# A two-layer attention block on one core: another order for layer 0's output projection of the first batch, and for vector work beside attention

## The chip, the cores and the metric

The kernel runs on one core of one Trainium2 chip. The metric is the time of one execution on the device, in microseconds (us), taken as the median of several runs. One execution was also recorded by the hardware profiler. The core has five engines, each of which works through its own queue in order: TensorE (PE, matrix products), VectorE (DVE), ScalarE (ACT), GpSimd (POOL), and SyncE (SP), which here only issues transfers. Engines wait for each other by semaphores.

## The reference, cut to what matters

The input `x` has 8 images of 32×32 positions with 512 channels, all in fp32. Two residual layers follow one another:

```python
x = x + L0(_gn(x), w_qkv, w_proj, b_proj)
x = x + L1(_gn(x), Wq, Wk, Wv, Wo, pos_emb_w, pos_emb_h)

def _gn(v, G=32, eps=1e-5):       # mean and variance over an image and 16 channels
    ...
def L0(x, w_qkv, w_proj, b_proj): # 16 heads of 32 channels, 1024 tokens
    q, k, v = split(x @ w_qkv)
    attn = softmax((q * 32 ** -0.5) @ k.T)
    return (attn @ v) @ w_proj + b_proj
def L1(x, Wq, Wk, Wv, Wo, pos_emb_w, pos_emb_h):  # 4 heads of 128 channels
    q, k, v = x @ Wq * 128 ** -0.5, x @ Wk, x @ Wv
    attn = softmax(q @ k.T + relative_logits(q, pos_emb_w, pos_emb_h))
    return (attn @ v) @ Wo
```

## The kernel before, in words

**Projections.** Every product with a 512×512 weight matrix is a Strassen-Winograd product: seven factor products of half size stand for eight. Four sums of blocks of the moving operand are needed for them, made on DVE by `forming` (lines 339 to 362; `forms` runs it through): s1 = a21 + a22, s2 = s1 − a11, a21 := a11 − a21, s4 = a12 − s2. Products 0 and 1 take a11 and a12 as they are, product 3 takes a22, and products 5, 4, 6 and 2 take s2, s1, the new a21 and s4. The like sums of the weights are made by POOL once at the start (`Matrix.add_up`) and stored to DRAM. A projection is done in two units u, one for each half of the output channels. `seven` (line 390) issues a unit: product 0 into the PSUM bank x, which ACT copies out as p1; product 5 into bank y, to which DVE adds p1, giving a (line 411); product 1 into x; product 4 into y, from which DVE makes b (line 419); product 6 into bank z, copied by ACT as p7; then products 2 and 3. A product that reuses a bank waits for the reader of what was there. Sinks take the results; the sink `Onto` adds them to the residual, with a POOL addition for the parts that come by a snapshot (line 502) and DVE additions for the others (lines 507 and 509). `two_first` and `five_last` (lines 437 to 475) issue products 0 and 1 of a unit and the other five apart; before, only the last batch's WO uses them.

**Layer 0's attention** (`attention_0`, line 595) goes over four groups of heads (m), two halves of the tokens (h) and eight blocks of keys (j). A step issues `front` of block j and then `back` of block j − 1. `front`: matmuls ps (line 603), then the exponential e on ACT (line 611). `back`: matmuls acc (line 622), then DVE's running sum es (line 631 for the first two blocks, line 633 for the others). ps has one PSUM buffer and e two, so that ACT's exponential of block j must wait until DVE has added block j − 2 to es, and the matmuls of block j + 1 must wait for that exponential. At the end of a half the sum over keys is made by a matmul (line 643), and the result normalised by ACT, DVE and at last POOL (line 588, q times su).

**What stands beside it.** The main loop goes through b = 0 to 8. Beside layer 0's attention of batch b it puts, in a chain: the output projection WP of batch b − 1 with its residual (`after_0`, line 891); layer 1's output projection WO of batch b − 2 (`after_1`), woven with the group norm of batch b − 1 (`norm_1`, line 905); layer 1 of batch b − 1 (`second`, line 910, projections Wq, Wk, Wv, and `attention_1`), woven with the loading and the group norm of batch b + 1 (`load`, line 786); and layer 0's projections of batch b + 1 (`before_0`). For the first batches, where some of these don't exist, the place is taken by others: `rest_of_first` finishes batch 0's projections beside the load of batch 1, and `other_keys` the second unit of batch 1's keys beside batch 0's norm.

A group norm is: statistics of a chunk of 128 channels (bn_stats, line 259; bn_aggr, line 260); a chain of DVE operations on a few columns ("small operations", lines 285 to 296, from `turned` to `var`); the power on POOL (line 300); four normalisations of 128×1024 (line 304). The residual is stored to DRAM before it is normalised (`put_away`, line 223, tile d) and fetched again for the next addition (`fetch`, line 232, into x1T or x2T).

**What sets the order.** All parts are generators, which yield after a piece of work with its cost in matmuls. `side_by_side` issues pieces of the chain beside the attention's steps in proportion to these costs. `woven(main, side, start, gap, places)` takes one piece of `side` at those pieces of `main` whose number, less `start`, leaves a remainder in `places` when divided by `gap`. In-order queues do the rest: the framework puts each engine's instructions in an order near that of issue, and `tc.issue_after(x)` keeps an instruction behind x. Weight factors come by SP (`Stream`, line 200 and 204) in the order of `plan`, seven factors ahead, through 16 buffers, and all other transfers of SP stand in the same queue.

Of the kernel before, what the change touches and what calls it, by code (L numbers as in the profile page):

```python
# [27 lines left out]
def quick_path(  # L28
# [23 lines left out]
    nc = tc.nc  # L52
# [265 lines left out]
    begun = [None]  # L318
    half_done = [None]

    added = [None]

    def by_columns(out, weights, moving, start, stop, open_sum=False):
# [12 lines left out]
                tc.keep_in_program_order(ins)  # L336
        in_place[0] = False

    def forming(x, name, room=None, behind=None):


        a11, a12 = x[:, :HC, :NB], x[:, HC:, :NB]
        a21, a22 = x[:, :HC, NB:], x[:, HC:, NB:]
        if room is not None:
            s1, s2, s4 = [room[:, i, :].rearrange("p (c n) -> p c n", n=NB) for i in range(3)]
        else:
            s1, s2, s4 = [
                mem.tile([P, HC, NB], F32, tag=f"form{i}", name=f"f{i}_{name}", bufs=1)
                for i in (1, 2, 4)
            ]  # L350
        for op, out, one, other in (
            (nc.vector.tensor_add, s1, a21, a22),
            (nc.vector.tensor_sub, s2, s1, a11),
            (nc.vector.tensor_sub, a21, a11, a21),
            (nc.vector.tensor_sub, s4, a12, s2),
        ):

            late = behind() if behind is not None else None
            with tc.issue_after(late.ins) if late is not None else nullcontext():
                last_form[0] = op(out, one, other)  # L360
            yield 0
        return [a11, a12, s4, a22, s1, s2, a21]

    def forms(x, name, room=None):
        got = []
# [31 lines left out]
    def seven(fs, u, rows, sink, name, hook=None):  # L397

        product = taken(fs, u, rows)
        x = bank(f"x_{name}")
        product(x, 0, True)
        p1 = snapshot("e1", f"p1_{name}")
        nc.scalar.copy(p1, x)
        yield HC
        y = bank(f"y_{name}")
        product(y, 5, True)
        a = snapshot("es1", f"a_{name}")  # L410
        begun[0] = nc.vector.tensor_add(a, y, p1)
        sink.early(p1, a)
        yield HC
        product(x, 1, False)
        sink.c11(x)
        yield HC
        product(y, 4, False)
        b = snapshot("es1", f"b_{name}")
        half_done[0] = nc.vector.tensor_add(b, y, p1)
        sink.middle(b)  # L420
        yield HC
        z = bank(f"z_{name}")
        product(z, 6, True)
        p7 = snapshot("e1", f"p7_{name}")
        nc.scalar.copy(p7, z)  # L425
        yield HC
        product(y, 2, False)
        sink.c12(y, p1)
        if hook is not None:
            hook()  # L430
        yield HC
        product(z, 3, False)
        sink.c21(z, a)
        sink.c22(b, p7)
        yield HC

    def two_first(fs, u, sink, name):

        product = taken(fs, u, False)
        x = bank(f"x_{name}")  # L440
        product(x, 0, True)
        p1 = snapshot("e1", f"p1_{name}")
        nc.scalar.copy(p1, x)
        product(x, 1, False)
        sink.c11(x)
        return p1

    def five_last(fs, u, sink, name, p1):
        product = taken(fs, u, False)
        y = bank(f"y_{name}")  # L450
        product(y, 5, True)
        a = snapshot("es1", f"a_{name}")
        nc.vector.tensor_add(a, y, p1)
        sink.early(p1, a)
        product(y, 4, False)
        b = snapshot("es1", f"b_{name}")
        nc.vector.tensor_add(b, y, p1)
        sink.middle(b)
        z = bank(f"z_{name}")
        product(z, 6, True)  # L460
        p7 = snapshot("e1", f"p7_{name}")
        nc.scalar.copy(p7, z)
        product(y, 2, False)
        sink.c12(y, p1)
        product(z, 3, False)
        sink.c21(z, a)
        sink.c22(b, p7)

    class Plain:

# [119 lines left out]
    def attention_0(q, k, v, b, blocks=range(NT)):  # L590
# [23 lines left out]
        def back(m, h, j, e):  # L614
            name = f"0_{b}_{m}_{h}_{j}"
            if j == blocks[0]:
                state["acc"] = psum.tile([P, NB], F32, tag="acc", name=f"acc_{name}", bufs=1)
                state["first"] = e
            acc = state["acc"]
            for r in range(HB):  # L620
                c0 = (m * HB + r) * D0
                nc.tensor.matmul(  # L622
                    acc[r * D0 : (r + 1) * D0, :],
                    v[:, j, c0 : c0 + D0],
                    e[:, r, :],
                    start=(j == blocks[0]),
                    stop=(j == blocks[-1]),
                )
            if j == blocks[1]:
                state["esum"] = mem.tile([P, HB, NB], F32, tag="es0", name=f"es_{name}", bufs=1)  # L630
                nc.vector.tensor_add(state["esum"], state["first"], e)  # L631
            elif j != blocks[0]:
                nc.vector.tensor_add(state["esum"], state["esum"], e)  # L633
            if j != blocks[-1]:
                return
            nc.scalar.copy(q[m][:, h * NB : (h + 1) * NB], acc)
            state["ended"] = (m, h, state["esum"])
# [149 lines left out]
    def load(b, st):  # L787
# [18 lines left out]
        yield 0  # L806
        st["kept"] = put_away(xT, f"0_{b}")
        yield from group_norm(st, xT, f"0_{b}")
        st["xn"] = yield from forming(x, f"xn0_{b}", behind=lambda: added[0])

    def load_first(st):

# [63 lines left out]
    def before_0(b, st, hook=None):  # L876
# [1 line left out]
        fs = st["xn"]  # L878
        st["q0"] = block(f"q0_{b}")
        st["q"] = chunks(st["q0"])  # L880
        yield from project_T(fs, WQ0, st["q"], f"q0_{b}")
        st["k"] = chunks(block(f"k0_{b}"))

        yield from project_T(fs, WK0, st["k"], f"k0_{b}", (0,) if b == 1 else (0, 1))
# [5 lines left out]

    def after_0(b, st, hook=None):

        fs = st.pop("ao0") if "ao0" in st else forms(st["q0"], f"ao0_{b}", block(f"forms_{b}"))
        x = st["x1"] = block(f"x1T_{b}")
        xT = fetch(st["kept"], x)
        for u in range(2):
            bias = [bproj_sb[:, n * HC + u : n * HC + u + 1] for n in range(2)]
            stream.unit(WP, False, u)
            yield from seven(
                fs, u, False, Onto(halves(xT, u), bias), f"wp_{b}_{u}", hook if u else None  # L900
            )
            for n in range(2):
                statistics(st, xT, n * HC + u, f"1_{b}")

    def norm_1(b, st, after=None, behind=None):
        xT = chunks(st["x1"])
        st["kept"] = put_away(xT, f"1_{b}")
        yield from group_norm(st, xT, f"1_{b}", after, behind)

    def second(b, st):  # L910

        fs = forms(st.pop("x1"), f"xn1_{b}")
        q = st["ao"] = block(f"q1_{b}")
        yield from project_T(fs, WQ1, chunks(q), f"q1_{b}")
        posT = block(f"posT_{b}", dtype=F32R)
        k = chunks(block(f"k1_{b}"))
        v = block(f"v1_{b}", [P, NT, C])
# [50 lines left out]
    def after_last(b, st):  # L968
# [1 line left out]
        x = st["ao"]  # L970
        xT = fetch(st["kept"], block(f"x2T_{b}"))
        sinks = [Onto(halves(xT, u), then=put_out(b, st, xT, u)) for u in range(2)]
        early = [x[:, :HC, :NB], x[:, HC:, :NB]]
        p1s = []
        for u in range(2):
            stream.unit(WO, False, u)
            p1s.append(two_first(early, u, sinks[u], f"wo_{b}_{u}"))
        fs = forms(x, f"ao1_{b}")
        for u in range(2):
            stream.unit(WO, False, u)  # L980
            five_last(fs, u, sinks[u], f"wo_{b}_{u}", p1s[u])

    def woven(main, side, start, gap, places=(0,)):

# [26 lines left out]
    def chain(*parts):  # L1011
        for part in parts:
            yield from part

    def marked():
        in_place[0] = True
        return
        yield
# [12 lines left out]
    def units(m, rows=False):  # L1031
        return [(m, rows, u, ORDER) for u in range(2)]

    FIRST = units(WQ0) + units(WK0) + units(WV0, True)
    plan = [(m, m is WV0, u, ORDER) for u in range(2) for m in (WV0, WQ0, WK0)]
    for b in range(B + 1):
        if b >= 1:
            plan += units(WP)
        if b == 1:
            plan += units(WK0)[1:]  # L1040
        if b >= 2:
# [2 lines left out]
            plan += units(WQ1) + units(WK1) + units(WV1, True)  # L1044
        if b + 1 < B:
            plan += FIRST if b else units(WQ0) + units(WK0)[:1] + units(WV0, True)
    plan += [(WO, False, u, some) for some in (FIRST_TWO, LAST_FIVE) for u in range(2)]

    states = [{} for _ in range(B)]
    load_first(states[0])  # L1050
# [21 lines left out]
    for b in range(B + 1):  # L1072
# [10 lines left out]

        if last is not None:
            if past is not None:
                norm = norm_1(b - 1, last, after=lambda: half_done[0])
            else:
                norm = norm_1(b - 1, last, behind=lambda: begun[0])
            rest.append(after_0(b - 1, last, forms_past if past is not None else None))
            total += PRODUCT  # L1090
            if past is not None:
                rest.append(woven(later(after_1, b - 2, past), norm, 3, 3))
                total += PRODUCT
            else:
                rest.append(chain(woven(other_keys(b, here), norm, 0, 1), marked()))
                total += PRODUCT // 2
            rest.append(later(second, b - 1, last))
            total += SECOND
# [14 lines left out]
                incoming = later(late_output, past)  # L1113
            rest.append(woven(attention, incoming, 4, 5))
        else:
            rest.append(woven(rest_of_first(here), incoming, 0, 2))
            total += PRODUCT
        if coming is not None:

# [502 lines left out]
```

## Time and profile before

| quantity | us |
|---|---|
| median of three runs | 3848.02 (3847.01 to 3848.98) |
| the profiled execution | 3848.35 |
| its span, first to last instruction | 3846.6 |
| PE busy | 3789.4 |
| DVE busy | 2555.1 |
| ACT busy | 1760.2 |
| POOL busy | 621.6 |

The span is what the trace covers; 1.75 us of the profiled execution lie around it. Busy shares are averages over the span. In a line of the timeline, the first number is the start from the span's beginning, the second the duration (of all instructions of the group, where x16 or the like stands behind it), then engine, line of the code, operation, output <- inputs with their shapes, and in brackets the idle time of the engine just before, with what ended it. In a line of waits: engine, what it issued <- what it waited for, the total in us, how many times, the longest. Batch 0's layer 0 runs up to about 310 us, and from b = 2 on one round of the main loop takes some 471 us.

### The profile page before, as it was taken

The numbers are of one execution on the slowest core, as the hardware profiler recorded it, in microseconds if no ns is written. First come the engines' busy times: TensorE is split into PE (matmuls) and PEld (weight loads), VectorE is DVE, ScalarE is ACT, GpSimd is POOL, SyncE is SP. The second block draws the span as 40 slices with busy tenths as digits, with TensorE's granted clock in tenths as the row PEclk, the third lists the DMA queues.
The fourth block names the chain that finished last, engine by engine and source line by source line (L and its number), as shares of the span: only waits on it lengthen the run. The fifth ranks groups of instructions, "written<-read, shape, count | busy, mean of one in ns | idle before, by whom it ended". The sixth has DMA issues, their size and how long they took to land.

```text
span 3846.6 us, 79883 instructions
## 1 busy us (share of the span) xinstructions
PE 3789.4 (99%) x34478; PEld 1376.3 (36%) x34478; DVE 2555.1 (66%) x2966; ACT 1760.2 (46%) x1830; POOL 621.6 (16%) x398
## 2 busy tenths in 40 slices
PE   9999999999999999999999999999999999999998
PEld 4222244222443234432343323433234332334353
DVE  6777775686755866558665686656866568665544
ACT  3554544545444454444544445444454445553132
POOL 1342101121011211012101121111210112001201
PEclk9999999999999999999999999999999999999999
DMA  6122120142202322023120241103311023110321
GB/s 185 61 88 81 41 59 6 44 122 62 56 9 83 89 54 56 13 92 85 45 55 16 93 93 38 50 21 98 90 40 41 26 96 78 33 37 31 109 41 26
DMA packets 482983, 234.72 MB, mean 61 GB/s; under 512 B 269600, under 2 KB 461376, under 8 KB 481600
## 3 DMA queue, kind: packets, MB, share of 16 engines
q1 hardware_dynamic: 470992, 213.74, 20.5%
q0 software_dynamic: 2608, 13.70, 1.0%
q8 instruction: 273, 4.47, 0.5%
q10 hardware_dynamic: 9024, 2.10, 0.3%
q14 instruction: 86, 0.70, 0.1%
HBM read 170.72 MB, written 58.72 MB: 60 GB/s over the span
## 4 chain that ended last, share of the span: by engine, by line
PE 88%; DVE 7%; ACT 2%; issue 2%; DMA 0%; SPq 0%; POOL 0%; DVEq 0%; ACTq 0%; POOLq 0%
PE ps L603 12%; PE ps L718 11%; PE acc L730 11%; PE acc L622 11%; PE y_q L327 4%; PE y_v L327 4%; PE y_k L327 4%; PE ps L719 3%; PE x_q L327 3%; PE x_v L327 3%; PE z_k L327 3%; PE x_k L327 3%; PE z_q L327 3%; PE z_v L327 3%; DVE es L633 2%; ACT e L611 2%
## 5 line engine op out<-in xcount | busy, mean ns | idle before, releaser
L611 ACT ACTIVATE e<-ps 128x2048 f32<-128x2048 f32 x512 | 961.7, 1878 | 840.1 <-PE ps L603 630.0
L633 DVE TENSOR_TENSOR es<-es,e 128x2048 f32<-128x2048 f32 x384 | 894.8, 2330 | 403.7 <-ACT e L611 400.4
L603 PE MATMUL ps<-q,k 32*64 32x512 f32 x8192 | 579.1, 614 | 17.1 <-ACT e L611 17.1
L622 PE MATMUL acc<-e,v 128*32 128x512 f32 x4096 | 546.7, 605 | 0.0
L721 ACT ACTIVATE e<-ps 128x512 f32<-128x512 f32 x512 | 305.7, 597 | 507.1 <-PE ps L719 436.4
L718 PE MATMUL ps<-q,k 128*128 128x512 f32 x1024 | 525.0, 594 | 0.2 <-DVE posT L704 0.2
L730 PE MATMUL acc<-e,v 128*128 128x512 f32 x1024 | 522.0, 593 | 0.3 <-ACT e L721 0.3
L588 POOL TENSOR_TENSOR q<-q,su 128x512 f32<-128x512 f32 x128 | 212.7, 1662 | 1550.3 <-DVE su L584 1427.7
L741 DVE TENSOR_TENSOR es<-es,e 128x512 f32<-128x512 f32 x384 | 290.4, 756 | 251.0 <-ACT e L721 248.4
L719 PE MATMUL ps<-posT,sel 128*128 128x512 f32 x512 | 406.6, 794 | 0.0
L718 PEld LDWEIGHTS ps<-q,k 128*128 128x128 f32 x1024 | 192.5, 190 | 230.1 <-issue 218.5
L603 PEld LDWEIGHTS ps<-q,k 32*64 32x64 f32 x8192 | 120.6, 130 | 410.1 <-issue 223.5
L730 PEld LDWEIGHTS acc<-e,v 128*128 128x128 f32 x1024 | 193.1, 189 | 147.3 <-issue 92.6
L622 PEld LDWEIGHTS acc<-e,v 128*32 128x32 f32 x4096 | 81.3, 108 | 412.7 <-issue 366.1
L631 DVE TENSOR_TENSOR es<-e,e 128x2048 f32<-128x2048 f32 x64 | 171.6, 2681 | 32.8 <-ACT e L611 32.7
L568 DVE STREAM_TRANSPOSE tu<-su 128x512 f32<-128x512 f32 x128 | 90.5, 707 | 97.3 <-ACT su L566 95.7
L719 PEld LDWEIGHTS ps<-posT,sel 128*128 128x128 f32 x512 | 97.3, 190 | 122.5 <-issue 122.5
L566 ACT COPY su<-sums 128x512 f32<-128x512 f32 x128 | 74.9, 585 | 131.2 <-PE sums L643 81.5
L704 DVE TENSOR_TENSOR posT<-pp,posT 32x512 fp32r<-32x512 f32 x128 | 112.0, 875 | 31.9 <-ACT posT L699 30.6
L492 POOL TENSOR_TENSOR k<-b_k,p_k 128x512 f32<-128x512 f32 x32 | 52.0, 1624 | 483.4 <-ACT p_k L425 472.7
L699 ACT CAST posT<-pp 32x512 fp32r<-32x512 f32 x128 | 105.9, 827 | 45.8 <-PE pp L686 44.7
L492 POOL TENSOR_TENSOR v<-b_v,p_v 128x512 f32<-128x512 f32 x32 | 51.6, 1614 | 433.9 <-ACT p_v L425 433.9
(214 smaller groups left out, 4546.0 us busy)
## 6 DMA issues: line engine op xcount, KB each, us to landing
w_qkv<-ws_qkv SPq DMA_DIRECT2D x168, 128.0 KB, 2.5
d<-x0T SPq DMA_DIRECT2D x32, 512.0 KB, 3.0
x1T<-d SPq DMA_DIRECT2D x32, 512.0 KB, 5.9
d<-x1T SPq DMA_DIRECT2D x32, 512.0 KB, 3.6
x2T<-d SPq DMA_DIRECT2D x32, 512.0 KB, 6.1
w_qkv<-in_L_conv_w_qkv SPq DMA_DIRECT2D x126, 128.0 KB, 2.2
out<-ot SPq DMA_DIRECT2D x240, 64.0 KB, 2.0
xs<-in_x SPq DMA_DIRECT2D x224, 64.0 KB, 2.5
```

Of the source, the lines that this page charges most:

```text
L327: ins = nc.tensor.matmul(out[columns, :], weights[:, columns], moving, start=start, stop=stop, skip_group_check=open_sum,)
L588: nc.gpsimd.tensor_tensor(dst, dst, su, op=ALU.mult)
L603: nc.tensor.matmul(ps[some, r, :], k[m][rows, j * P + 64 * i : j * P + 64 * i + 64], q[m][rows, h * NB : (h + 1) * NB], start=True, stop=True,
L611: nc.scalar.activation(e, ps, AF.Exp, scale=D0 ** -0.5)
L622: nc.tensor.matmul(acc[r * D0 : (r + 1) * D0, :], v[:, j, c0 : c0 + D0], e[:, r, :], start=(j == blocks[0]), stop=(j == blocks[-1]),)
L631: nc.vector.tensor_add(state["esum"], state["first"], e)
L633: nc.vector.tensor_add(state["esum"], state["esum"], e)
L718: nc.tensor.matmul(ps, k[h][:, keys], q[:, h, queries], start=True, stop=False)
L719: nc.tensor.matmul(ps, sel_flat[:, keys], posT[:, h, queries], start=False, stop=True)
L721: nc.scalar.activation(e, ps, AF.Exp, scale=1.0 / math.sqrt(D1))
L730: nc.tensor.matmul(acc, v[:, j, h * D1 : (h + 1) * D1], e, start=(j == 0), stop=(j == NT - 1),)
L741: added[0] = nc.vector.tensor_add(state["esum"], state["esum"], e)
```

## The change

What each part of the edit does:

- A new generator, `in_two_parts`, issues products 0 and 1 of both units ahead of products 5, 4, 6, 2 and 3 of both. The last batch's WO had this order before, written out in `after_last`, which now calls it; the first batch's WP has it now too. There x1T is fetched ahead of the sums; `forming`'s first two sums are woven with the first products, the last two with the fives of unit 0; each sum is kept behind the attention's last es (`summed`); and the statistics of a unit (`done`) come behind the next a (`begun`).
- `reader` is the last a or b made. While `beside_norm` is set, an addition to es is kept behind it. It is set for batch 0's WP, and for `after_1` woven with the norm.
- The norm's small operations go behind a `summed` (b = 1) or, as before, `half_done` (from b = 2 on); from b = 2 on the four normalisations are also kept behind `summed`; the norm's pieces are taken at other places of `after_1`.
- From b = 2 on, the first two of layer 1's four sums are made at the end of the norm (`sums_1`), and the last two within the projection Wq (`second`). For batch 1's first load (`load`), the first three sums are made at once, in a fixed order to es and b, and the last within the projection WQ0 of `before_0`.
- The plan of weights follows the new order for the first WP.

```diff
+    def in_two_parts(x, m, sinks, name, room=None, done=lambda u: None, behind=None):
+        early = [x[:, :HC, :NB], x[:, HC:, :NB]]
+        p1s, fs = [], []
+        sums = forming(x, name, room, behind, fs)
+        def products():
+            for u in range(2):
+                stream.unit(m, False, u)
+                p1s.append((yield from two_first(early, u, sinks[u], f"{name}_{u}")))
+        def beside(u):
+            if u == 0:
+                yield from sums
+                return
+            with tc.issue_after(begun[0].ins):
+                done(0)
+            yield 0
+        yield from woven(products(), (next(sums) for _ in range(2)), 0, 1)
+        for u in range(2):
+            stream.unit(m, False, u)
+            yield from woven(five_last(fs, u, sinks[u], f"{name}_{u}", p1s[u]), beside(u), 0, 1)
+        done(1)
...
@@ attention_0, back
+            if j != blocks[0]:
+                with tc.issue_after(reader[0].ins) if beside_norm[0] else nullcontext():
+                    summed[0] = nc.vector.tensor_add(state["esum"], other, e)
...
@@ load
-        st["xn"] = yield from forming(x, f"xn0_{b}", behind=lambda: added[0])
+        if b > 1:
+            st["xn"] = yield from forming(x, f"xn0_{b}", behind=lambda: added[0])
+            return
+        fs = st["xn"] = []
+        done, read = lambda: summed[0], lambda: half_done[0]
+        sums = st["sums0"] = forming(x, f"xn0_{b}", behind=(done, read, read, done), into=fs)
+        yield next(sums)
+        yield 0
+        for _ in range(2):
+            yield next(sums)
...
@@ before_0
-        yield from project_T(fs, WQ0, st["q"], f"q0_{b}")
+        yield from woven(
+            project_T(fs, WQ0, st["q"], f"q0_{b}"), st.pop("sums0", iter(())), 0, 2 * len(ORDER)
+        )
...
@@ after_0
-        fs = st.pop("ao0") if "ao0" in st else forms(st["q0"], f"ao0_{b}", block(f"forms_{b}"))
         x = st["x1"] = block(f"x1T_{b}")
         xT = fetch(st["kept"], x)
+        def done(u):
+            def look(u=u):
+                for n in range(2):
+                    statistics(st, xT, n * HC + u, f"1_{b}")
+            if b == B - 1 and u:
+                st["look"] = look
+            else:
+                look()
+        if "ao0" not in st:
+            yield from in_two_parts(
+                st["q0"], WP, sinks, f"wp_{b}", block(f"forms_{b}"), done, lambda: summed[0]
+            )
+            return
...
@@ norm_1, sums_1 and second
+        if "look" in st:
+            with tc.issue_after(begun[0].ins):
+                st.pop("look")()
...
+    def sums_1(b, st):
+        fs = st["xn1"] = []
+        done = lambda: summed[0]
+        sums = st["sums1"] = forming(
+            st.pop("x1"), f"xn1_{b}", behind=(done, done, done, lambda: half_done[0]), into=fs
+        )
+        for _ in range(2):
+            yield next(sums)
...
-        yield from project_T(fs, WQ1, chunks(q), f"q1_{b}")
+        yield from woven(project_T(fs, WQ1, chunks(q), f"q1_{b}"), sums, 0, 2 * len(ORDER), (0, 3))
...
+    def with_norm(part):
+        beside_norm[0] = True
+        yield from part
+        beside_norm[0] = False
...
+    def in_parts(m):
+        return [(m, False, u, some) for some in (FIRST_TWO, LAST_FIVE) for u in range(2)]
...
-            plan += units(WP)
+            plan += units(WP) if b > 1 else in_parts(WP)
...
@@ the main loop
-                norm = norm_1(b - 1, last, after=lambda: half_done[0])
+                norm = norm_1(
+                    b - 1, last, after=lambda: half_done[0], behind=lambda: summed[0]
+                )
+                if coming is not None:
+                    norm = chain(norm, later(sums_1, b - 1, last))
             else:
-                norm = norm_1(b - 1, last, behind=lambda: begun[0])
-            rest.append(after_0(b - 1, last, forms_past if past is not None else None))
+                norm = norm_1(b - 1, last, after=lambda: summed[0], behind=lambda: begun[0])
+            first = after_0(b - 1, last, forms_past if past is not None else None)
+            rest.append(first if past is not None else with_norm(first))
             if past is not None:
-                rest.append(woven(later(after_1, b - 2, past), norm, 3, 3))
+                rest.append(with_norm(woven(later(after_1, b - 2, past), norm, 3, 14, (0, 3, 6, 8, 9))))
             else:
-                rest.append(chain(woven(other_keys(b, here), norm, 0, 1), marked()))
+                rest.append(chain(woven(other_keys(b, here), norm, 1, 1), marked()))
...
-            rest.append(woven(rest_of_first(here), incoming, 0, 2))
+            rest.append(woven(rest_of_first(here), incoming, 0, 1))
```

## The prediction

> **What bounds the kernel.** First the page's list of busy time:
>
> ```profile
> PE 3789.4 (99%) x34478; PEld 1376.3 (36%) x34478; DVE 2555.1 (66%) x2966; ACT 1760.2 (46%) x1830; POOL 621.6 (16%) x398
> ```
>
> TensorE's own instructions set the time, and the change leaves their number and kinds alone. All it can win is the 57.2 us of the 3846.6 us span in which PE isn't busy. The view of waits says what PE waited for (total, times, longest, in us):
>
> ```profile
> PE ps L603 <- ACT e L611: 17.1, 16, 2.9
> PE y_wo L327 <- DVE a_wo L411: 9.1, 6, 1.8
> ...
> PE sums L643 <- DVE es L633: 3.1, 2, 1.8
> PE y_wp L327 <- DVE forms L360: 2.5, 1, 2.5
> ```
>
> These are the places that the diff touches. Since ends of matmuls are modelled, I measure a stall from start to start against undisturbed neighbours: a product takes 1.72, eight ps 1.05, eight acc 0.88 to 1.0. The timeline shows batches 2 to 6 alike; this is one (start, duration, engine, line, operation, and the idle time before it):
>
> ```profile
> 1314.33 2.98 DVE L304 TENSOR_SCALAR x1T<-x1T,back,rstd 128x1024 f32<-128x1024 f32 x4 [1.20 <-POOL rstd L300]
> 1317.23 2.28 DVE L633 TENSOR_TENSOR es<-es,e 128x2048 f32<-128x2048 f32 x1
> ...
> 1319.60 1.88 ACT L611 ACTIVATE e<-ps 128x2048 f32<-128x2048 f32 x1 [5.25 <-DVE es L633]
> 1321.54 1.12 PE L603 MATMUL ps<-q,k 32*64 32x512 f32 x16 [0.98 <-ACT e L611]
> ...
> 1325.24 4.64 DVE L633 TENSOR_TENSOR es<-es,e 128x2048 f32<-128x2048 f32 x2
> ...
> 1329.80 0.68 DVE L411 TENSOR_TENSOR a_wo<-y_wo,p_wo 128x512 f32<-128x512 f32 x1
> 1330.54 1.92 PE L327 MATMUL y_wo<-f_ao,w_o 128*32 128x512 f32 x16 [1.42 <-DVE a_wo L411]
> ```
>
> The reader is to see two queues on DVE. Four normalisations (2.98) hold up an addition to es; ACT can't write the next e before that, nor PE the next ps: start 1321.54, due at 1320.48, 1.06 lost. Then two es (4.64) hold up a_wo, which frees PE's accumulator: start 1330.54, due at 1328.94, 1.60 lost. Batch 0's output projection:
>
> ```profile
> 322.69 1.26 POOL L588 TENSOR_TENSOR q<-q,su 128x512 f32<-128x512 f32 x1 [19.78 <-DVE su L584]
> 322.96 1.07 PE L603 MATMUL ps<-q,k 32*64 32x512 f32 x2 [1.04 <-ACT e L611]
> 323.99 1.22 DVE L360 TENSOR_TENSOR forms<-q 128x1024 f32<-128x1024 f32 x1 [1.44 <-POOL q L588]
> 325.25 1.23 DVE L360 TENSOR_TENSOR forms<-forms,q 128x1024 f32<-128x1024 f32 x1
> ...
> 326.53 2.94 PE L327 MATMUL y_wp<-forms,w_p 128*32 128x512 f32 x16 [2.50 <-DVE forms L360]
> ```
>
> PE waits 1.46 for ps and 3.43 for the sums, start to start, and y_wp then takes 2.94, not 1.90. The view by stretches (busy times, then granted clock, DMA share, GB/s) explains the last:
>
> ```profile
> 141.00:146.00 5.00, 4.83 (x60) 1.18 (x61) 3.93 (x2) 2.47 (x3) 4.35 (x2) 1.00 0.60 223
> ...
> 320.00:331.00 11.00, 7.46 (x52) 1.21 (x45) 7.95 (x12) 2.46 (x2) 1.98 (x2) 0.84 0.57 210
> ```
>
> Against the same groups elsewhere, 320 to 331 loses 2.6 to the clock (1.04 in y_wp, 0.61 in the ps behind it, the rest further on): 7.5 in all.
>
> **The change, part by part.**
>
> *Batches 2 to 6.* Readers (a_wo, b_wo) go ahead of es additions, the norm's small operations behind one, and the four normalisations are split two and two. I walked DVE's new order with the old durations. a_wo of unit 0 now runs at 1302.3, so es ends 0.68 later and e at 1307.15, where PE wants it at 1307.50: hidden, by 0.3. With two normalisations ahead of it, es lets e end at 1319.8 (wanted 1320.48). a_wo of unit 1 ends at 1327.0 (wanted 1327.88). Layer 1's third and fourth sums follow later than before but keep 1.4 to their products. So both stalls go: the five batches show 1.06 five times, 1.60 four times and 1.77 once, 13.5. Bounds 8 (one wait of the three with thin slack comes back) to 14.5.
>
> *Batch 0's output projection (320 to 348).* PE does both units' products 0 and 1, which need no sums, before the fives: two more products, 3.44, lie over the wait for sums. DVE puts the first two sums ahead of es and the rest behind; four statistics (4×0.69 + 2×0.2 = 3.2) move past a_wp. POOL adds p_wp (1.27) ahead of q·su for unit 0 and right behind it for unit 1. New waits by the walk: 0.1 and about 0.4 at two ps; 0.75 where unit 1's product 4 stands only one ps matmul behind product 5 and wants a_wp: product 5 must end, and DVE's 0.69 follow, before PE goes on. Left 1.25 of 7.5.
> Two rules bear on this.
> The first speaks against it. In the 128x1024 rows a sum took 1.22 alone, but 2.29 at 130.39 under a POOL addition (1.41), and two es took 9.38 for 4.6 beside POOL work at 156.08. "SBUF — State Buffer", section "Who interferes with whom", says that a DVE instruction with two SBUF inputs contends with a POOL instruction that reads SBUF; unit 1's addition now starts together with the first sum. By the row of sums alone (1.22) the ps wait is 0.4, by rule and second row (the sum 0.8 to 1.1 longer) 1.1. I take 0.85: left 1.7, gain 5.8.
> In the second they differ. "TensorE: Matmul & The Clock Gate", "What's actually happening", gives the half clock only after an idle window of about 3.4 us. PE's idle times here are 1.04 and 2.50 with work between; by the rule there is no slow clock to win back, this part is 3.2 and the whole sum 19.4. The row has clock 0.84 and y_wp at 2.94, so I count it; what stays (at most 1.1 each) is under the shortest wait that a slow stretch follows in this trace (1.82, at 165.6), though one of 1.85 at 376 had none. Bounds 2 to 7.5.
>
> *Batch 1's norm, behind it.* At 376.34 PE waited for e (1.92 start to start), because small operations (369.43 to 372.1) stood ahead of es. Now they follow it: gain 1.6 of it, since es still ends 0.3 late. The norm, and with it the store of x1T and layer 1's sums, comes some 2.3 later; the four normalisations ended at 382.1, the second sum at 387.3, and PE first reads them in x_q at 392.97 and y_q at 396.73: hidden by 9, and PE's loss beyond that. Bounds 0 to 1.9.
>
> *Batch 1's load.*
>
> ```profile
> 134.94 2.00 DVE L360 TENSOR_TENSOR f_xn<-x0T,f_xn 128x1024 f32<-128x1024 f32 x1
> 136.87 2.28 DVE L631 TENSOR_TENSOR es<-e,e 128x2048 f32<-128x2048 f32 x1
> ...
> 141.17 1.12 PE L603 MATMUL ps<-q,k 32*64 32x512 f32 x16 [2.92 <-ACT e L611]
> ```
>
> The fourth sum (2.00) moves behind the next es: ps could start 2 earlier. But b_k goes behind a sum and an es, to 129.45, where product 2 wanted it at 127.97: a new wait of 1.45, behind which all PE work is queued. ps lands 0.6 to 1.2 earlier; the sum then sits in DVE gaps (0.56 and 0.92) before the es of 156.08. Net 0.75, bounds −1.5 to 2.5.
>
> *Batches 7 and 8.* At 3214.35 a wait of 1.31 goes, but a_wo now delays the es of 3217.9, and most is lost at 3222.8: 0.35 (−0.5 to 1.5). In batch 8 a wait of 1.62 at 3575.9 goes for one of 0.5 behind four statistics, and the rest at the norm: 0 (±0.7). The last batch's WO keeps its order.
>
> *SP and the DMAs.* Four fetches of x1T (landing 4.1 to 6.7 after issue at 322.4) go from behind 18 weight transfers to third. Their buffer is that of POOL's sum of w_o, whose store (issued 270.7, landing after 4.3) they must await: SP stands from 273.1 to about 275.6, and every w_p behind it comes 2.5 later, but is used from 308: hidden. ACT's copy p_wp of unit 1 goes ahead of an exp, 0.58, inside the 0.1 above. Stores of d and out move by one place; nothing on the chip reads them soon. Without that cover each us would be PE's.
>
> Sum: 13.5 + 5.8 + 1.6 + 0.75 + 0.35 + 0 = 22.0. Span 3846.6 − 22.0 = 3824.6. The profiled execution took 3848.35, 1.75 more than its span; the median, 3848.02, is 0.33 under it: 3826.0.
>
> **Rivals.**
> 1. *The wait moves.* In batches 2 to 6 the slack is 0.3 at 1307.5; if DVE is later than in my walk (es took 2.53 there beside POOL), PE loses about 1.1 per batch again, or 1.6; this part is 5.5 to 8, the sum 14 to 16.5: about 3833. For it: slack is thin at three places. Against: the durations of these rows repeat in five batches.
> 2. *Sharing and clock.* POOL beside the sums, and the new waits of 1.45 and 0.75, slow the clock again: batches 0 and 1 yield 2 in place of 8: about 3832. For it: clock 0.84 after 1.82. Against: 1.00 in 141 to 146, right after 2.92.
> 3. *Slower.* x1T third in SP's queue waits for the store; POOL, in order, stands at p_wp with q·su behind it, and the sums and PE behind that. Landing at about 275.6 + 2.4 + 6.7 = 285, it has 38 us until 322.7. To lose 0.2% net it must pay 22 + 7.7 = 30: landing after 353, 68 late. No DMA row comes near: 3856 if so.
> 4. *Nothing.* The releasers named were not the true ones (a DMA, say), and the stalls stay: 3848. Against: start times follow es + 1.88 in every case.
>
> **How the numbers follow.** Likeliest 0.62, with its own range 3820 to 3831 from the bounds (not all at an end at once); rival 1 0.17, rival 2 0.11, rival 3 0.03, rival 4 0.05; 0.02 for a larger gain. 0.2% is 7.7 us, about what a measurement can tell from no change. Faster: 0.62 + 0.17 + 0.11 + 0.02 = 0.92; same 0.05; slower 0.03. The range takes in rivals 1 and 2: 3818 to 3835.
>
> **What would show it.** Right: y_wo<-a_wo gone from the waits, ps<-e down from 17.1 to about 5; y_wp without a wait for the forms and no stretch at 0.84 there; batch period (1321.54 − 850.32 = 471.2) shorter by 2.7. Wrong: that period unchanged, or a wait of about 1 at ps two blocks after a_wo (rival 1); y_wp or ps groups of 1.7 and more near 130 or 325 (rival 2); POOL waiting for DMA at 322 (rival 3).

## The result, and the profile after

The changed kernel takes 3826.55 us in the median (3825.92 to 3826.70, six runs) against 3847.34 of the kernel before on the same chip (3846.50 to 3848.98, six runs): a ratio of 0.9945, 95% interval 0.9932 to 0.9958. The prediction was 3826.0. The span of the profiled execution is 3824.8, 21.8 shorter than before. The total agrees to 0.55 us, but two terms of the sum were off by 2 to 3 us each, in opposite directions. The experiments below look into that.

First the page's busy time, of the changed kernel:

```profile
PE 3786.5 (99%) x34478; PEld 1377.5 (36%) x34478; DVE 2564.1 (67%) x2966; ACT 1761.1 (46%) x1830; POOL 658.5 (17%) x398
```

The instruction counts are the same. POOL is busy 37 us longer with the same 398 instructions, and DVE 9 us longer: more of them now stand beside one another and take longer there (an addition x2T<-x2T,b_wo took 1.28 at 1310.38 before and 3.35 at 1296.24 now, under an es). The waits of PE:

```profile
PE ps L645 <- ACT e L653: 11.3, 15, 1.5
...
PE y_wo L331 <- DVE a_wo L464: 1.0, 1, 1.0
...
PE y_wo L331 <- DVE a_wo L420: 0.7, 1, 0.7
...
PE y_k L331 <- DVE b_k L428: 0.4, 1, 0.4
```

(Lines 603, 611 and 411 of before are now 645, 653 and 420.) The wait of y_wo for a_wo fell from 9.1 to 0.7; the waits for the forms and of sums for es are gone from the list. The wait of ps for e is still 11.3, where about 5 had been expected. A new one for b_k is there.

Since PE does the same work in nearly the same order, the two traces can be laid side by side: at every matmul group that has its like in the other, the difference of the two start times says how far ahead the changed kernel is. A step in that difference is time won or lost: a wait, a slow clock, or matmuls that no longer run side by side. The steps, read at the ps and sums, and positive where the changed kernel gains:

| stretch | prediction's sum | step, before to after |
|---|---|---|
| up to 98 us, where the order is the same | 0 | −0.4 |
| batch 1's load, 98 to 199 us | 0.75 | 4.0 (−1.4, +2.2, +2.0, +1.2) |
| batch 0's output projection | 5.8 | 5.3 |
| the norm behind it | 1.6 | 1.25 |
| batches 2 to 6 | 13.5 | 11.1 (2.17, 2.15, 2.50, 2.16, 2.16) |
| batches 7 and 8 | 0.35 | 0.4 (+1.50, −1.29, +0.23) |

What is left to 21.8 is in steps of 0.35 and less elsewhere. The −1.4 of the load is the new wait for b_k; first the ps behind it before, then the changed kernel:

```profile
130.67 1.11 PE L603 MATMUL ps<-q,k 32*64 32x512 f32 x16
```

```profile
129.78 1.47 PE L331 MATMUL y_k<-f_xn,prep_qkv 128*32 128x512 f32 x9 [0.38 <-DVE b_k L428]
...
132.47 1.11 PE L645 MATMUL ps<-q,k 32*64 32x512 f32 x16
```

The changed kernel was 0.39 behind ahead of this place and is 1.80 behind at this ps. Only 0.6 of the 1.41 is there at the first matmul of sums, ahead of that ps; the rest is lost because matmuls of y_k that ran beside those of z_k before now come late, among those of sums. At 141 us the ps then gains 2.22, at 163 the sums 2.00.

The timeline of the changed kernel in one of batches 2 to 6, the same batch as was shown of before:

```profile
1290.15 0.65 DVE L420 TENSOR_TENSOR a_wo<-y_wo,p_wo 128x512 f32<-128x512 f32 x1
1290.37 1.28 POOL L630 TENSOR_TENSOR q<-q,su 128x512 f32<-128x512 f32 x1 [11.55 <-DVE su L626]
1290.72 3.08 DVE L679 TENSOR_TENSOR es<-e,e 128x2048 f32<-128x2048 f32 x1
...
1293.92 1.88 ACT L653 ACTIVATE e<-ps 128x2048 f32<-128x2048 f32 x1 [5.05 <-DVE es L679]
...
1295.85 1.12 PE L645 MATMUL ps<-q,k 32*64 32x512 f32 x16 [0.45 <-ACT e L653]
...
1304.17 1.54 DVE L304 TENSOR_SCALAR x1T<-x1T,back,rstd 128x1024 f32<-128x1024 f32 x2 [0.31 <-POOL rstd L300]
...
1314.44 0.68 DVE L420 TENSOR_TENSOR a_wo<-y_wo,p_wo 128x512 f32<-128x512 f32 x1
...
1316.24 1.90 PE L331 MATMUL y_wo<-f_ao,w_o 128*32 128x512 f32 x16
```

The normalisations stand two and two, a_wo comes in time, and both old stalls are gone: the steps there are 1.06 and 1.60. But a new one of 0.52 stands at 1295.85: the es ahead of it took 3.08, not the 2.25 of before. Batch 0's output projection:

```profile
318.89 1.28 POOL L630 TENSOR_TENSOR q<-q,su 128x512 f32<-128x512 f32 x1 [6.65 <-DVE su L626]
...
320.20 1.23 DVE L369 TENSOR_TENSOR forms<-q 128x1024 f32<-128x1024 f32 x1 [0.82 <-POOL q L630]
...
321.46 2.19 DVE L369 TENSOR_TENSOR forms<-forms,q 128x1024 f32<-128x1024 f32 x1
...
326.28 1.90 PE L331 MATMUL y_wp<-forms,w_p 128*32 128x512 f32 x14
...
344.86 1.07 PE L645 MATMUL ps<-q,k 32*64 32x512 f32 x2
345.86 1.92 PE L331 MATMUL y_wp<-forms,w_p 128*32 128x512 f32 x16
```

PE doesn't wait for the sums any more. The second sum took 2.19 beside POOL's addition, but with two more products under it that was hidden. The view by stretches has clock 1.00 here (the third number from the end is the granted clock, ahead of DMA share and GB/s):

```profile
322.00:333.00 11.00, 11.00 (x116) 2.61 (x112) 10.41 (x7) 4.62 (x3) 3.82 (x2) 1.00 0.09 26
```

### The profile page after: what moved, and what is told of

Same layout as the page of the kernel before. It is cut to its first block, busy times and chain, and to the rows that moved or that the text cites. A ratio compares the mean times of both kernels' runs of the same rounds, so it can differ in the third digit from the quotient of the medians.

```text
span 3824.8 us, 79906 instructions
## 1 busy us (share of the span) xinstructions
PE 3786.5 (99%) x34478; PEld 1377.5 (36%) x34478; DVE 2564.1 (67%) x2966; ACT 1761.1 (46%) x1830; POOL 658.5 (17%) x398
## 4 chain that ended last, share of the span: by engine, by line
PE 92%; DVE 4%; ACT 2%; issue 1%; DMA 0%; SPq 0%; POOL 0%; DVEq 0%; ACTq 0%; POOLq 0%
PE ps L645 13%; PE acc L664 12%; PE ps L764 12%; PE acc L776 12%; PE y_q L331 4%; PE y_v L331 4%; PE y_k L331 4%; PE ps L765 3%; PE x_q L331 3%; PE x_v L331 3%; PE z_k L331 3%; PE z_q L331 3%; PE x_k L331 3%; PE z_v L331 3%; ACT e L653 2%; DVE es L679 2%
## 5 line engine op out<-in xcount | busy, mean ns | idle before, releaser
L645 PE MATMUL ps<-q,k 32*64 32x512 f32 x8192 | 577.7, 613 | 11.3 <-ACT e L653 11.3
L630 POOL TENSOR_TENSOR q<-q,su 128x512 f32<-128x512 f32 x128 | 201.6, 1575 | 1536.2 <-DVE su L626 1412.1
```

What stands on the lines that cost most here:

```text
L630: nc.gpsimd.tensor_tensor(dst, dst, su, op=ALU.mult)
L645: nc.tensor.matmul(ps[some, r, :], k[m][rows, j * P + 64 * i : j * P + 64 * i + 64], q[m][rows, h * NB : (h + 1) * NB], start=True, stop=True,
```

## The experiments

Each changes only what its diff shows; except where said, no engine but DVE has another order than the changed kernel. Ratios are to the kernel before, measured beside each. Steps are differences of start times against the changed kernel's trace, positive where the run is later.

**Batch 1's load in the old order.**

```diff
-        if b > 1:
+        if b > 0:
             st["xn"] = yield from forming(x, f"xn0_{b}", behind=lambda: added[0])
...
-            rest.append(woven(rest_of_first(here), incoming, 0, 1))
+            rest.append(woven(rest_of_first(here), incoming, 0, 2))
```

> The changed kernel with two DVE instructions of batch 1's load put back: b_k ahead of the first sum's neighbour, the fourth sum ahead of es. Theory L (the load is worth what the two traces show between 130 and 199 us, 3.6): about 3.6 us slower than the changed kernel (3830.1), with a wait of sums for es of about 1.8 near 165 us and a granted clock of about 0.84 behind it. Theory S (the load is worth the 0.75 of the prediction's sum, and the rest of the 3.6 came from elsewhere): 3827.3, and no such wait.

Measured: 3830.31 (3828.90 to 3830.54), ratio 0.9954 (0.9937 to 0.9970), 3.8 above the changed kernel. The steps are −1.42 by the ps near 131 us (b_k's wait isn't there), +2.22 at the ps near 141 and +2.00 at the sums near 165. Waits between 90 and 200 us, and the stretch around the wait of sums:

```profile
PE ps L603 <- ACT e L611: 3.9, 3, 2.9
PE sums L643 <- DVE es L633: 1.8, 1, 1.8
```

```profile
160.00:171.00 11.00, 9.18 (x84) 2.00 (x84) 7.73 (x8) 4.82 (x4) 4.26 (x3) 0.84 0.35 122
```

```profile
PE ps L645 <- ACT e L653: 4.2, 3, 2.9
PE sums L689 <- DVE es L679: 1.8, 1, 1.8
```

```profile
160.00:171.00 11.00, 9.18 (x105) 2.24 (x104) 9.10 (x10) 4.82 (x4) 4.40 (x4) 1.00 0.34 125
```

The first two fences are the kernel before, the other two this one. Theory L holds for the wait: two DVE instructions bring it back. It fails for the clock: with the same wait of 1.8 before it, this stretch has clock 1.00, where before had 0.84, so this trace is only 2.8 (−1.4, +2.2 and +2.0) behind the changed kernel. The profiled execution took 3828.90, the other three 3830.11 to 3830.54; whether those had the slow clock isn't shown.

**The same with POOL not reading.** Why are the es near 156 us slow?

```diff
-                    engine.tensor_tensor(sums[:, i], x, y, op=ALU.subtract)
+                    if self.name == "q1":
+                        engine.memset(sums[:, i], 0.0)
+                    else:
+                        engine.tensor_tensor(sums[:, i], x, y, op=ALU.subtract)
```

> The kernel of the run with the old order in batch 1's load, and in it the four POOL subtractions of 128x512 that make the weight sums of Wq are four fills with zero of the same tiles, so that POOL writes there but reads nothing (layer 1's q is then not the reference's: a probe of time alone). Theory R (DVE's es and POOL's subtractions hold each other up because both read SBUF): the two es near 156 us take about 4.6 in place of 9.4, and the 1.8 wait of sums near 165 is gone, as it is in the changed kernel. Rival (es was late for another reason: the place of the fourth sum, or ACT): 9 and 1.8 stay.

One execution: 3828.75. (Lines 645, 653 and 679 are 648, 656 and 682 here.) The timeline of the kernel before at this place, and of this run:

```profile
156.08 9.38 DVE L633 TENSOR_TENSOR es<-es,e 128x2048 f32<-128x2048 f32 x2
156.23 3.76 POOL L152 TENSOR_TENSOR prep_q<-prep_q 128x512 f32<-128x512 f32 x3
```

```profile
158.07 2.28 DVE L682 TENSOR_TENSOR es<-es,e 128x2048 f32<-128x2048 f32 x1
...
161.33 2.29 DVE L682 TENSOR_TENSOR es<-es,e 128x2048 f32<-128x2048 f32 x1 [0.97 <-ACT e L656]
...
165.60 1.05 PE L692 MATMUL sums<-es,ones 128*32 128x512 f32 x8
```

Theory R: 2.28 and 2.29, and sums wait for nothing. (A fill takes 0.52 where a subtraction took 1.28, so POOL is done earlier too, and no fill stands beside either of these es. That reading is what counts shows in an es at 150.66: it took 2.87, 0.6 more than alone, until a subtraction that began at 150.10 was over, and nothing for the fills at 151.31 and 152.36 under it.) That the time is no shorter has another cause, in the same trace: behind the wait of 2.92 that ends at 141.74 the clock is slow, which it wasn't in the kernel before or in the run above after the same wait:

```profile
141.74 2.01 PE L648 MATMUL ps<-q,k 32*64 32x512 f32 x16 [2.92 <-ACT e L656]
...
143.68 1.60 PE L667 MATMUL acc<-e,v 128*32 128x512 f32 x8
```

```profile
141.00:146.00 5.00, 4.26 (x36) 1.00 (x40) 2.47 (x2) 2.56 (x2) 3.59 (x2) 0.66 0.72 243
```

1.44 lost there, start to start. In the changed kernel POOL's subtractions and DVE's es still stand side by side, but the fourth sum has moved in between, and now POOL is the one that is held up:

```profile
154.77 9.31 POOL L152 TENSOR_TENSOR prep_q<-prep_q 128x512 f32<-128x512 f32 x3
...
156.90 6.04 DVE L679 TENSOR_TENSOR es<-es,e 128x2048 f32<-128x2048 f32 x2
...
163.19 1.05 PE L689 MATMUL sums<-es,ones 128*32 128x512 f32 x8
```

Before, three subtractions took 3.76 and two es 9.38; now 9.31 and 6.04. That the two hold each other up is shown; why it falls so differently isn't. In the changed kernel they take turns. Before, the first es was recorded 0.16 ahead of the first subtraction and still ended 2.16 after the third, at 162.16, while no subtraction was held up (1.28 each).

**b_k first.** Of the load's two moves, undo b_k's alone.

```diff
-        sums = st["sums0"] = forming(x, f"xn0_{b}", behind=(done, read, read, done), into=fs)
+        sums = st["sums0"] = forming(x, f"xn0_{b}", behind=(read, read, read, done), into=fs)
+        yield 0
+        yield 0
         yield next(sums)
-        yield 0
```

> The changed kernel, but b_k of batch 1's load goes ahead of the first sum again; nothing else moves. Theory: the wait of y_k for b_k near 129 us (0.6 from start to start against before; my sum had 1.45) goes, the wait of sums near 163 doesn't come back, since the fourth sum stays where the change put it: about 0.6 faster than the changed kernel. Rival (it was b_k's move that cured the wait of sums): 2.8 to 3.4 slower, with that wait back.

3825.91 (3825.18 to 3826.49), ratio 0.9944 (0.9928 to 0.9959). The step by the ps near 131 us is −1.41, not the 0.60 that was expected and that stands at the sums before it; but 1.08 is given back at the ps near 141, since the es it waits for, now earlier, meets more of POOL's q times su (it takes 3.07, in the changed kernel 2.63). The wait of sums stays away: it is the fourth sum's move that cured it. What is left in the traces, 0.3, is too little for the times to tell: the medians differ by the 0.6 expected, but the ranges overlap.

**Batch 0's output projection in one part.**

```diff
-        if "ao0" not in st:
-            yield from in_two_parts(
-                st["q0"], WP, sinks, f"wp_{b}", block(f"forms_{b}"), done, lambda: summed[0]
-            )
-            return
-        fs = st.pop("ao0")
+        fs = st.pop("ao0") if "ao0" in st else forms(st["q0"], f"ao0_{b}", block(f"forms_{b}"))
...
-            plan += units(WP) if b > 1 else in_parts(WP)
+            plan += units(WP)
```

Here PE and SP have the old order too, and so have a few instructions of ACT and POOL. The additions to es stay behind the readers.

> The changed kernel with batch 0's output projection in the old order of products (a whole unit, then the other). Theory L: about 5.3 us slower than the changed kernel (3831.9), with a wait of about 2.5 for the sums, y_wp's first product at about 2.9 in place of 1.9 and a granted clock under 0.9 around it. Rival (the additions' new order beside it did the work, not the two more products): less than 2 us slower, and the wait for the sums short.

3832.66 (3831.63 to 3833.87), ratio 0.9959 (0.9945 to 0.9974): 6.1 above the changed kernel, and a step of 6.75 in the traces. Its timeline and stretch:

```profile
324.01 3.64 PE L331 MATMUL y_wp<-forms,w_p 128*32 128x512 f32 x16 [2.96 <-DVE forms L369]
```

```profile
322.00:333.00 11.00, 8.99 (x60) 1.78 (x60) 6.36 (x7) 1.88 (x1) 1.27 (x1) 0.69 0.06 13
```

The two more products did the work, and the slow clock is part of what they save: y_wp's product lost 1.75 and the ps behind it 0.88, start to start, where before it was 1.04 and 0.61. With the wait for the sums, 2.96 for 2.50, that is the 1.45 by which 6.75 is above 5.3. The rival falls.

**Batch 0's norm ahead of es.**

```diff
-                norm = norm_1(b - 1, last, after=lambda: summed[0], behind=lambda: begun[0])
+                norm = norm_1(b - 1, last, behind=lambda: begun[0])
...
-                rest.append(chain(woven(other_keys(b, here), norm, 1, 1), marked()))
+                rest.append(chain(woven(other_keys(b, here), norm, 0, 1), marked()))
```

> The changed kernel, but the small operations of batch 0's norm stand ahead of the first es of the half again, as before. Theory: ps waits near 366 us for about 1.9 from start to start in place of 0.68, so everything behind it comes about 1.2 later than in the changed kernel (prediction's sum: 1.6). Rival: POOL's q times su, which starts just ahead of that es and holds it up to 3.03, sets the wait: then no more than 0.3 later.

One execution, 3827.56 (a fill of POOL changes places here too); the step is 1.26, and the wait of ps for e in 340 to 380 us is 1.9, as before. The es took 2.29 here, not the 3.03 of the changed kernel, since POOL's q times su was over by then. So the norm set the wait, and the changed kernel loses some of its gain because its es meets q times su.

**Batches 2 to 8 in the old order.**

```diff
-                norm = norm_1(
-                    b - 1, last, after=lambda: half_done[0], behind=lambda: summed[0]
-                )
-                if coming is not None:
-                    norm = chain(norm, later(sums_1, b - 1, last))
+                norm = norm_1(b - 1, last, after=lambda: half_done[0])
...
-                rest.append(with_norm(woven(later(after_1, b - 2, past), norm, 3, 14, (0, 3, 6, 8, 9))))
+                rest.append(woven(later(after_1, b - 2, past), norm, 3, 3))
...
-            if b == B - 1 and u:
+            if False:
```

SP's order follows that of DVE here.

> The changed kernel with DVE's order of batches 2 to 8 as before. Theory L: about 11.3 us slower than the changed kernel (five times 2.17 to 2.5, 0.2 and 0.2): 3837.9; waits of y_wo for a_wo back at 9. Theory S (the prediction's 13.5 + 0.35): 3840.4. Rival (most of the gain came from the first two batches): under 8 slower.

3838.48 (3836.93 to 3840.62), ratio 0.9976 (0.9966 to 0.9985): 11.9 above the changed kernel. The steps are 2.46, 2.16, 2.17, 2.16 and 2.16, then 1.49 and −1.28. Theory L holds and the sum's 13.85 doesn't. All moves of these batches are undone together; which of them cured what is read from the places of the steps, 1.06 at the ps behind the normalisations and 1.6 at the y_wo behind a_wo. The old wait is back:

```profile
PE y_wo L331 <- DVE a_wo L420: 8.7, 6, 1.6
```

**The first es ahead of a_wo.** What takes 0.52 in each of these batches?

```diff
-                with tc.issue_after(reader[0].ins) if beside_norm[0] else nullcontext():
+                with tc.issue_after(reader[0].ins) if beside_norm[0] and j != blocks[1] else nullcontext():
```

> The changed kernel, but the first addition of an es goes ahead of a_wo again (batches 2 to 6 unit 0, batch 7 unit 1); nothing else moves on any engine. Theory W (a_wo ahead lets POOL's q times su start before the es, which then took 3.08 in place of 2.25 and made ps wait 0.52 in each of five batches and 1.29 in batch 7): those waits go, about 3.9 us faster than the changed kernel (3822.7). Rival (the waits come from ACT's e or from the later additions): within 1 us of the changed kernel. Second rival (a_wo behind es makes y_wo wait again): slower by up to 5 times 1.6.

3825.17 (3824.24 to 3827.83), ratio 0.9939 (0.9923 to 0.9956): 1.4 below the changed kernel, between theory W and its rival. The same place as above:

```profile
1292.74 2.25 DVE L679 TENSOR_TENSOR es<-e,e 128x2048 f32<-128x2048 f32 x1
1292.96 3.18 POOL L630 TENSOR_TENSOR q<-q,su 128x512 f32<-128x512 f32 x1 [11.55 <-DVE su L626]
...
1294.91 0.68 DVE L420 TENSOR_TENSOR a_wo<-y_wo,p_wo 128x512 f32<-128x512 f32 x1
...
1297.93 1.11 PE L645 MATMUL ps<-q,k 32*64 32x512 f32 x16
```

es and q times su have changed places: here the one that starts first takes its 2.25 or 1.28, and the other one pays (3.18 or 3.08). The step at this ps is −0.52 in all five batches, and −1.38 in batch 7: the waits go, as W has it. But 0.31 of it comes back 42 us later:

```profile
1338.92 0.67 DVE L420 TENSOR_TENSOR a_q<-y_q,p_q 128x512 f32<-128x512 f32 x1
...
1339.65 1.92 PE L331 MATMUL y_q<-f_xn,w_q 128*32 128x512 f32 x16
```

PE comes 0.52 earlier to a place where DVE doesn't: a_q ends a row of DVE instructions without a gap, which stand 2.60 later than in the changed kernel's trace, as PE did ahead of this ps (this trace has a late start). PE is now 2.08 later, and y_q waits for a_q. In batch 7 0.41 comes back there and 0.47 at the sums.

**All three together.**

```diff
-        yield from woven(project_T(fs, WQ1, chunks(q), f"q1_{b}"), sums, 0, 2 * len(ORDER), (0, 3))
+        part = woven(project_T(fs, WQ1, chunks(q), f"q1_{b}"), sums, 0, 2 * len(ORDER), (0, 3))
+        for at, cost in enumerate(part):
+            beside_norm[0] = 0 < b < B - 1 and at < 2
+            yield cost
+        beside_norm[0] = False
```

with the edits of the runs with b_k first and with the first es free. The b of this cut is layer 1's batch, one less than the main loop's.

> Three moves on DVE together, nothing else: the first es of a half ahead of a_wo (as in the run with that es free), b_k first, and in batches 1 to 6 a_q of unit 0 ahead of the es behind it, since the run with that es free gave 0.31 of its 0.52 per batch back in a wait of y_q for a_q. Theory: 5 times 0.52, 1.38 and 0.6, about 4.5 faster than the changed kernel, if the other waits of batch 7 (0.41 and 0.47) go too, 3.6 if they stay: about 3822.5 to 3823. Rival (PE's next wait takes it back each time): 3825 or more, as in the run with that es free.

3823.21 (3822.67 to 3824.28), ratio 0.9937 (0.9923 to 0.9951). All five runs are below all six of the changed kernel, by 3.3 in the medians, with the kernel before at 3847.25 and 3847.34 beside them; the traces show 3.2 behind 98 us. Now a_q comes at 1333.01, y_q at 1335.60 without a wait, and each of the five batches keeps its 0.52. In batch 7 the 1.39 that goes is taken back at its sums (1.10): there the es that a_q was put ahead of is one of the half's last, and sums waits for ACT's q and es. So this is faster than both kernels, but by three small moves that each paid only where the next reader had room.

## Why the prediction was right, and where it wasn't

*Batches 2 to 6.* Both stalls, their sizes (1.06 and 1.60) and their causes were right: the steps are the same to 0.02. What failed is "hidden, by 0.3". The walk took es with the duration of before, 2.25 to 2.28. With a_wo ahead of it, POOL's q times su started first, es took 3.08, and e was 0.5 too late: 0.52 five times is 2.6, and 13.5 − 2.6 = 10.9 against the 11.1 measured. This is rival 1 at half its price, and the rule that the prediction had weighed at batch 0 alone (the Trainium skill, "SBUF — State Buffer", section "Who interferes with whom": a DVE instruction with two SBUF inputs contends with a POOL instruction that reads SBUF). It should have been asked at each es that was moved, above all where the slack was 0.3. The page's section "SBUF: two separate sides" also says who pays: of two such instructions, the one that starts first has the ports that they share for its whole length, and the other one waits. The pairs 2.25 and 3.18, 3.08 and 1.28 agree; the es at 156.08 of the kernel before, which was recorded first and still waited for three subtractions, doesn't, and no run here says why.

*Batch 0's output projection.* Right in kind, 5.3 for 5.8, but by two errors that nearly cancelled. The loss before was 5.3, not 7.5: from start to start 1.1 for e and 2.6 for the sums (the lines show idle times of 1.04 and 2.50), and 1.04 and 0.61 of slow clock in y_wp and the ps behind it. The prediction's "rest further on" of the clock (0.95) can't be found. Its 3.43 for the sums has 0.87 in it that isn't a wait: the row has only two of the ps matmuls ahead of y_wp, and those two took 1.07, about what sixteen take together, since they didn't run side by side; 0.3 of its 1.46 for e comes in the same way from x_wp's last six. On the other side, the 1.7 of new waits didn't come. The second sum did take 2.19, as the rule had it, but stood under the added products, and the ps ran without a wait. At unit 1's product 4, where 0.75 was taken, two ps matmuls stand alone again (344.86, taking 1.07) and y_wp follows 1.00 behind them, with no idle time shown: the split ps costs there what it cost before at 322.96, and a_wp, ended by 345.69, was in time. So nearly all that was lost here was won. That the clock's share is real is shown by the run in one part, with 0.69 in that stretch; by the idle window of about 3.4 us of "TensorE: Matmul & The Clock Gate", section "What's actually happening", neither kernel should have slowed, with idle times of 2.50 and 2.96.

*The norm behind it.* 1.25 for 1.6. The es was taken at 2.28 and was 3.03, again beside q times su.

*Batch 1's load.* This is the step that failed: 0.75, bounds up to 2.5, and 4.0 measured. As far as the ps at 141 us the working was right: the new wait for b_k cost 1.41 for the 1.45 worked out, and that ps came 0.80 earlier for "0.6 to 1.2". What was wrong is that the wait of sums at 165.60 and the slow clock behind it were taken to stay, since the fourth sum went into gaps of DVE just ahead of the two slow es. But those es were slow by contention, and their place against POOL's subtractions changed: 9.38 became 6.04, the wait of 2.00 (start to start) went, and with it the slow clock of that trace, 1.2 net. The prediction had quoted the 9.38 and its cause, and then treated it as a constant.

*Batches 7 and 8, SP and DMAs.* 0.35 and 0 came to 0.4. The fetch of x1T waited for the store as worked out: the store was issued at 266.92 and took 4.2, SP's fetch began at 271.22, landing after 5.8, and the first w_p behind it was issued at 273.09, when before had 273.11, though the kernel is 3.8 ahead by then. POOL first used x1T at 310.22. Nothing waited; rival 3 falls, and rival 4 with the steps.

Added up, the load gave 3.3 more, batches 2 to 6 gave 2.4 less, and batch 0 with its norm 0.9 less. The median was met because these cancel. The likeliest case was the right one; that it came within 0.55 us was luck.

## What to carry to other kernels

In this kernel a walk through an in-order engine with old durations was good to a tenth where no GpSimd instruction stood beside the ones that were moved. Wherever an edit moves a two-input VectorE instruction, even by less than a microsecond, look at which GpSimd instruction stands beside it and work the sum both ways, each of the two waiting for the other, since that alone moved 0.8 to 3.3 us of VectorE's time here. A stall read from start to start is only a stall where the matmuls between run side by side as elsewhere: hold it against the idle time that the profile shows. And a wait removed on the bounding engine brings it earlier to the next place: follow it there until the other engines have room, or it is given back.

## What the runs showed of the hardware that was not expected

The same idle time of PE did and did not slow its clock. Behind a wait of 2.92 at 141 us the granted clock was 1.00 in the kernel before and in the run with the old load, and 0.66 in the run without POOL's reads (1.44 us lost); behind 1.82 at 165 us it was 0.84 before, with about 1.5 us lost in the two groups behind it, and 1.00 in the run with the old load. "TensorE: Matmul & The Clock Gate", section "What's actually happening", says that the window in which activity is counted is free-running; that fits a dependence on where the wait falls, but no run here moved a wait against it on purpose, so it stays an inference. For a forecast of this kernel it means that a clock's share in a wait of 1.8 to 3 us is a chance of 1.4 to 2.6 us, the losses found here, and not a term.

Two executions can also differ at the very start: the profiled one of the run with the first es free reached 101 us 2.5 us later than the changed kernel's, with the same order up to there, and its time is the highest of its four.
